# Quarter additions on GpSimd between gathers, and a slot's work in two steps, in a two-layer graph network kernel

## The chip, the cores and the metric

The kernel runs on one core of a Trainium2 chip. Time is the device time of one launch in microseconds (us), the median of several runs: 2489.55 us before the change, over 11 runs from 2482.47 to 2493.50. Engines are named as in the profile: PE is the matrix engine (PEld its weight loads), DVE the vector engine, ACT the scalar engine, POOL is GpSimd, SP the engine that only issues DMAs.

## The reference

6250 nodes with 512 features, 100000 edges sorted by destination, eight heads of 64 features. Two layers, each added to its input:

```python
h = jnp.maximum(_layernorm(x, axis=-1), 0.0)
# edge layer 0: attention
h = leaky_relu(h @ W.T + b, 0.2).reshape(N, 8, 64)
e = leaky_relu(e_src[src] + e_dst[dst], 0.2)      # e_* : sums of h times a weight, per head
ex = jnp.exp(e - segment_max(e, dst)[dst])
a = ex / segment_sum(ex, dst)[dst] * dist
x = x + segment_sum(h[src] * a[:, :, None], dst)
h = jnp.maximum(_layernorm(x, axis=-1), 0.0)
# edge layer 1: mean of neighbours
neigh = segment_sum(h[src], dst) / deg
y = h @ W_self.T + neigh @ W_neigh.T + bias
x = x + _layernorm(y) * gamma + beta
```

## The kernel before

A prologue computes `h` and the two logit terms for 49 tiles of 128 nodes and stores rows of 520 numbers in DRAM. Then come the two edge layers, the bulk of the time.

**Edges.** The edge list is cut into four streams (q = 0 to 3), and each stream into 66 windows of three tiles (j = 0 to 2) of 128 edges. In each window twelve tiles are gathered: an indirect DMA on GpSimd's queue fetches, for 128 edges, the rows of their sources. GpSimd runs its instructions in the order in which they are written; a gather is an instruction on it like an addition. In the first layer (`gather`, L744) the rows land in `gbuf`, a ring of four windows: the gather for window k+4 overwrites the buffer of window k, tile by tile, once PE has used that tile. In the second (`gather1`, L1296) the tiles of half a window land in a ring of five.

**Products.** PE turns gathered rows into sums per destination with one-hot matrices (`add_up`, L1010; `add_up1`, L1325), adds what is carried from the window before (`finish`), and ACT copies the result out (`evac`), from where SP stores it.

**Messages (first layer).** Before PE uses a tile, its rows are multiplied in place by the attention weights: by DVE two streams at a time for the tiles j = 0 and 1 (`message`, L967), for the third tile in part by DVE (`message_part`, L974) and in groups of four heads by ACT (`message_act`, L986, four 128x64 activations a group). The upper four heads of streams 1 and 3 in that tile are left to GpSimd (`message_pool`, L998, steps `K0` and `K1`, one 128x256 multiplication each), except in the last two full windows.

**Order.** All engines' instructions are written out by hand: for each window k the list `ORDER` is gone through, and each name calls a function for window k plus an offset (`STEPS`). GpSimd's part of a window is K0, six gathers of window k+4 (`GA`), K1, the other six (`GB`). The tiles follow in the order `TILES` (stream, tile): 10 01 00 30 11 20 02 22 12 21 31 32.

**Slots.** 128 finished rows are a slot. Slots follow some windows (six windows of every seven, from window 9 on; 49 of them, of which the last belongs with six further ones to a late group that is handled at the end of a layer). In the first layer `slot_load` fetches the sums (`sa`) and the input (`sx`) of the slot of window k-2; `slot_run`, for the slot of window k-3, goes on by one step at each `S` of the order: divides by the softmax sums (DVE, L1088), adds `sx` and `sa` (DVE, 128x512, L1090), takes statistics (L1101), scales and stores the normalised rows. In the second layer `slot1_run` does the two dense products and the closing normalisation; its last lines add `beta` to `sx` (L1475), multiply by `gamma` (L1477) and add (L1478), on DVE but for the last two slots before the late ones.

**Buffers.** `sa0` has two buffers in the first layer, `sx` three; the penalties that separate destinations in the softmax (`penb`) four, loaded by `load_edges` four windows ahead.

Of the kernel before, what the change touches and what calls it, by code (L numbers as in the profile page):

```python
# [1 line left out]

# [17 lines left out]
NQ = 4  # L20
# [24 lines left out]
def gnn_kernel(ctx, tc, x, srcp, dstp, attrp, wt0, b0, wsrc, wdst, wts, wtn, bias1, gamma1, beta1, out):  # L45
# [673 lines left out]
    gp = lay0.enter_context(tc.tile_pool(name="gp", bufs=1))  # L719
    penb = [gp.tile([NQ * H, T * 128 + 1], FT, name=f"penb{i}") for i in range(4)]  # L720
    gbuf = gp.tile([128, NB, NQ, T, RW], FT, name="gbuf")
# [13 lines left out]

    def gather(k, part=None):
        GT[k] = g_ = gbuf[:, k % NB]
        tiles = [(q, j) for q, j in TILES if j < njof(k)]
        if k >= NW - 3:
            tiles.sort(key=lambda t: t[1])  # L740
        n = len(tiles) // 2
        for q, j in tiles if part is None else (tiles[:n], tiles[n:])[part]:
            c = k * T + j
            G.indirect_dma_start(out=g_[:, q, j, :], out_offset=None, in_=h0_d,  # L744
                                 in_offset=bass.IndirectOffsetOnAxis(ap=idx[:, q, c:c + 1], axis=0))

    def attr_turn(k, h):
# [24 lines left out]
    def load_edges(k):  # L772
        n = njof(k) * 128
        for p in (1, 0):
            if p == 0 and k % GRP[1]:
                continue
            eb = ed_tile(k, p)
            for q2 in range(2):
                S.dma_start(eb[64 * q2:64 * q2 + 64, (2 * p + q2) * H:(2 * p + q2 + 1) * H], ed_d[ds(base(k, 2 * p + q2), M), :])
        PEN[k] = pn = penb[k % 4]  # L780
        S.dma_start(pn[:, 0:n + 1], pen_d[:, k * T * 128:k * T * 128 + n + 1])
# [211 lines left out]

    def message_pool(k, p):

        if njof(k) == T and not (p and k in IDLE):
            x3 = GT[k][:, 2 * p + 1, T - 1, D // 2:D].rearrange("p (h d) -> p h d", d=D // H)
            G.tensor_tensor(out=x3, in0=x3, in1=A2[k][:, T - 1, 2 * p + 1, H // 2:H].unsqueeze(2).to_broadcast([128, H // 2, D // H]),  # L998
                            op=OP.mult)

    def add_up(k, p, j):
# [70 lines left out]
    def slot_load(s, r=None):  # L1072
        if r is None:
            r = load(tab[0:1, s:s + 1], NP - 128)
        sa = lp.tile([128, AW], FT, name="sa0")
        S.dma_start(sa, acc0_d[ds(r, 128), :])
        sx = lp.tile([128, D], FT, name="sx", bufs=3) if s + 1 != LATE[0] else keep[:, LATES]
        S.dma_start(sx, x[ds(r, 128), :])
        SA[s] = (r, sa, sx)
# [12 lines left out]

    def slot_run(s, engs=(V, V)):
        r, sa, sx = SA.pop(s)
        V.tensor_scalar(slc[:, s, 0:H + 1], sa[:, D:AW], 1.0, None, op0=OP.max)
        yield
        V.reciprocal(slc[:, s, 0:H + 1], slc[:, s, 0:H + 1])
        yield
        yield from residual(s, sa, sx, engs)
        s6 = lp.tile([128, 6], FT, name="s6_0")  # L1100
        V.bn_stats(s6, sx)  # L1101
        yield
        mv = lp.tile([128, 2], FT, name="mv_0")
        V.bn_aggr(mv, s6)
        yield
        y = yield from rstd_of(lp, mv[:, 1:2], 1, "s0", slc[:, s, 9:10])
        V.scalar_tensor_tensor(slc[:, s, 10:11], mv[:, 0:1], -1.0, y, op0=OP.mult, op1=OP.mult)
        yield
        A.activation(sx, sx, AF.Relu, scale=y, bias=slc[:, s, 10:11])
        if s + 1 == LATE[0]:  # L1110
            DONE.append((r, sx))
        else:
            S.dma_start(h1_d[ds(r, 128), :], sx)
# [38 lines left out]

    def ahead(k, part):
        if k >= NB - 1:
            gather(k, part)


# [10 lines left out]
        A10=(0, add_up, 1, 0), A11=(0, add_up, 1, 1), A12=(0, add_up, 1, 2), C0=(0, finish, 0), C1=(0, finish, 1),  # L1168
        EV0=(0, evac0), EV1=(-1, evac1), OH=(4, onehot), CS=(0, later(carry_sel)),
        GA=(NB, ahead, 0), GB=(NB, ahead, 1), K0=(0, message_pool, 0), K1=(0, message_pool, 1))  # L1170
    STEPS.update({f"H{p}{i}": (0, message_act, p, i) for p in range(2) for i in range(4) if p or i})
    ORDER = """
    K0 H01 D0b S D0a D1a TE ECb H11 NX S SCR S FT1 A00 D0c FL EV1 SV S H12 RESC A01 AT0 H02 OH TM A10 GA K1 S CM FDf
    A02 FX S RS S LM RH AT0c CS SSb C0 SUB PF L FT1c S EZ EXP D1b SCF S A11 H10 AT1 ECa AT1c FT0 S AA F9a S A12 F9b S
    EV0 FD SSa C1 FT0c S GB
    """.split()
# [8 lines left out]
    for k in range(-4, NW + 1):  # L1185
        sl_ = slot_run(slot(k - 3)) if slot(k - 3) is not None and slot(k - 3) not in LATE else none()
        c, kk = divmod(k, CH)
        when(k + 4, load_edges)
        if slot(k - 2) is not None and slot(k - 2) not in LATE:
            slot_load(slot(k - 2))  # L1190
        if kk == CH - 6 and 0 <= k and (c + 1) * CH < NW:
            attr_load(c + 1)
        for name in ORDER:
            if name[0:2] == "AT":
                (attr_copy if name[3:] else attr_turn)(k, 4 * int(name[2]))
            elif name == "S":
                step(sl_)
            elif name == "L":
                step(last)
            else:  # L1200
                d, f, *a = STEPS[name]
                when(k + d, f, *a)
        if NW - 6 < k <= NW - 2:
            for i in range(2 * (k - NW + 5), min(2 * (k - NW + 6), LATES)):
                late_x(i)
        last = sl_


    late_sa = gbuf[:, (NW - 4) % NB].rearrange("p q j r -> p (q j r)")[:, 0:LATES * AW].rearrange("p (i c) -> p i c", c=AW)
    for i, s_ in enumerate(LATE):  # L1210
        S.dma_start(late_sa[:, i], acc0_d[ds(ROW[s_], 128), :])
    run(last)
    for r, hs in DONE:
# [77 lines left out]
    def gather1(k, p):  # L1291
        GT[k, p] = g_ = ring[:, (2 * k + p) % 5]
        for j in range(njof(k)):
            for q2 in (1, 0):
                c = k * T + j
                G.indirect_dma_start(out=g_[:, q2, j, :], out_offset=None, in_=h1_d[0:NT * 128, :],  # L1296
                                     in_offset=bass.IndirectOffsetOnAxis(ap=idx[:, 2 * p + q2, c:c + 1], axis=0))

    lay1 = ExitStack()
# [133 lines left out]
    def slot1_mean(s):  # L1433
        sa = SA[s][3]
        if s not in OWN:
            A.activation(sa, sa, AF.Copy, scale=slc[:, s, 8:9])

    def slot1_run(s):
        r, hs, sx, sa = SA.pop(s)
# [34 lines left out]
        eng = G if LATE[0] - 2 <= s < LATE[0] else V  # L1474
        eng.tensor_tensor(out=sx, in0=sx, in1=gb[:, 1], op=OP.add)  # L1475
        yield
# [93 lines left out]
    STEPS1.update({f"A{p}{j}": (0, add_up1, p, j) for p in range(2) for j in range(T)})  # L1570
    SLOTS1 = dict(MEAN=(-2, slot1_mean), SUMS=(-1, slot1_sums))
    ORDER1 = """
    en en la MEAN A00 A01 A02 la A10 CS0 C0 EV1 OH en PUT en PRE G1 sl la SEL en en SUMS CS1 sl A11 A12 EV0 G0 C1 sl
    """.split()

    last, ends = none(), none()
    for k in range(-1, NW - 1):
# [5 lines left out]
        for name in ORDER1:  # L1583
# [14 lines left out]
            elif k >= 0 or name[0] != "G":  # L1598
                d, f, *a = STEPS1[name]
                when(k + d, f, *a)  # L1600
        if 12 <= k < 12 + NLATE:
            late_beta(k - 12)
# [192 lines left out]
```

## Time and profile before

| | |
|---|---|
| median of 11 runs | 2489.55 us |
| profiled execution, own time | 2492.52 us |
| its span, first to last instruction | 2490.7 us |
| granted clock of PE, mean | 0.923 |
| first layer, first gather's start to last gather's end | 225.8 to 1327.7 us |
| second layer, the same | 1406.5 to 2425.6 us |

The profile is of one execution. A group's row has the line, the engine, the operation, its output and inputs with shapes, the count, the busy time and the mean of one, and the idle time of that engine just before, with what ended it ("issue" is idle time in which the engine waited for nothing that the profile shows). The timeline has one row for each instruction or run of like ones.

### The profile page before, as it was taken

To read this page: it belongs to the slowest core of one execution; us is meant where nothing else is said; L and a number is where in the kernel's file an instruction comes from. 1 tells how busy PE (TensorE), PEld (TensorE's weight loads), DVE (VectorE), ACT (ScalarE), POOL (GpSimd) and SP (SyncE) were. 2 spreads that over 40 slices of the span, in tenths; PEclk is the share of its full clock that TensorE was granted. 3 is DMA by queue.
4 is the path that set the end of the run, shared out by engine and by line. 5 is a ranking of instruction groups with operands and counts; after the bars stand their busy time and mean duration, and the time that the engine had idled before them with its cause. 6 is when DMAs were issued, how large, how long until landed. Compare 5 with 4: busy or idle time off the path is not lost.

```text
span 2490.7 us, 32878 instructions
## 1 busy us (share of the span) xinstructions
PE 2068.6 (83%) x8780; PEld 1017.9 (41%) x8780; DVE 1539.4 (62%) x3120; ACT 984.9 (40%) x2957; POOL 1813.9 (73%) x1803
## 2 busy tenths in 40 slices
PE   7985799888888888898889277898888879888885
PEld 5774244333333333343334033344444434444344
DVE  7877566676867776867778422365545545555545
ACT  6862344555545555545554311222222222222212
POOL 5665777777777777777774477777777777777773
PEclk9997799999999999999999599899989999999898
DMA  6735777788888888888886688888888888888882
GB/s 208 226 92 158 211 220 213 233 271 242 260 257 262 255 261 258 256 257 250 258 254 189 212 250 256 269 284 281 282 276 288 284 276 285 281 284 277 289 272 85
DMA packets 264702, 611.54 MB, mean 246 GB/s; under 512 B 63604, under 2 KB 74372, under 8 KB 264510
## 3 DMA queue, kind: packets, MB, share of 16 engines
q0 software_dynamic: 125440, 414.35, 55.8%
q1 hardware_dynamic: 138494, 193.97, 23.6%
q8 instruction: 72, 1.18, 0.2%
q14 instruction: 120, 0.98, 0.1%
q10 hardware_dynamic: 576, 1.05, 0.1%
HBM read 511.44 MB, written 97.76 MB: 245 GB/s over the span
## 4 chain that ended last, share of the span: by engine, by line
PE 32%; DMA 22%; POOL 21%; issue 13%; DVE 8%; ACT 3%; SPq 1%; POOLq 0%; ACTq 0%; DVEq 0%
DMA g<-h_d,idx 15%; POOL gbuf L744 11%; POOL g L1296 8%; PE ps_w L1010 7%; PE ps_w L1325 4%; DMA gbuf<-h_d,idx 4%; PE ps_z L818 3%; PE ps_f L592 3%; PE ps_s L1325 2%; PE ps_b L592 2%; PE ps_w L592 2%; POOL gbuf L998 1%; PE ps_w L1027 1%; PE ps_z L827 1%; PE ps_f L1018 1%
## 5 line engine op out<-in xcount | busy, mean ns | idle before, releaser
L744 POOL DMA_INDIRECT gbuf<-h_d,idx x784 | 781.4, 997 | 249.1 <-issue 154.3
L1296 POOL DMA_INDIRECT g<-h_d,idx x784 | 780.5, 996 | 243.3 <-issue 182.5
L1010 PE MATMUL ps_w<-gbuf,oh 128*64 128x512 f32 x1568 | 491.6, 630 | 126.4 <-POOL gbuf L998 105.0
L986 ACT ACTIVATE gbuf<-gbuf,aa 128x64 f32<-128x64 f32 x1276 | 329.6, 334 | 1.6
L1325 PE MATMUL ps_s<-g,oh 128*64 128x512 f32 x784 | 213.2, 659 | 123.0 <-DMA g<-h_d,idx 75.3
L967 DVE TENSOR_TENSOR gbuf<-gbuf,ps_c 128x1024 f32<-128x1024 f32 x260 | 308.4, 1215 | 0.3 <-issue 0.3
L1325 PE MATMUL ps_w<-g,oh 128*64 128x512 f32 x784 | 219.0, 650 | 78.0 <-DMA g<-h_d,idx 77.3
L1010 PEld LDWEIGHTS ps_w<-gbuf,oh 128*64 128x64 f32 x1568 | 97.4, 137 | 249.6 <-POOL gbuf L998 179.2
L854 DVE TENSOR_TENSOR_SCAN nx<-penb,ms,ps_z 32x256 f32<-32x256 f32 x66 | 48.2, 730 | 208.2 <-PE ps_z L827 199.2
L1423 ACT ACTIVATE hs<-sx,slc 128x512 f32<-128x512 f32 x45 | 36.6, 814 | 352.8 <-PE ps_t L1406 212.7
L628 POOL TENSOR_TENSOR pr<-hr,watt 128x1024 f32<-128x1024 f32 x47 | 113.2, 2411 | 77.6 <-DVE hr L625 71.1
L1038 ACT ACTIVATE ws<-ps_w 128x512 f32<-128x512 f32 x103 | 60.6, 588 | 272.3 <-PE ps_w L1027 270.1
L1325 PEld LDWEIGHTS ps_s<-g,oh 128*64 128x64 f32 x784 | 47.9, 143 | 245.2 <-DMA g<-h_d,idx 135.1
L1412 DVE TENSOR_TENSOR lo<-ps_t,hi 128x512 fp32r<-128x512 f32 x55 | 38.0, 690 | 158.0 <-ACT hi L1411 157.5
L787 DVE TENSOR_TENSOR oh<-ps_c,dsr 128x768 f32<-128x768 f32 x130 | 123.0, 947 | 0.1
L818 PE MATMUL ps_z<-oht,edb 128*32 128x384 f32 (+1 forms) x264 | 121.6, 593 | 1.1 <-DVE mf L847 1.1
L1325 PEld LDWEIGHTS ps_w<-g,oh 128*64 128x64 f32 x784 | 43.0, 140 | 182.6 <-DMA g<-h_d,idx 127.4
L1027 PE MATMUL ps_w<-ws,cs 128*128 128x512 f32 x170 | 97.3, 654 | 0.0
L998 POOL TENSOR_TENSOR gbuf<-gbuf,aa 128x256 f32<-128x256 f32 x128 | 82.2, 643 | 19.3 <-DVE slc L198 17.2
L1345 ACT ACTIVATE ws<-ps_w 128x512 f32<-128x512 f32 x66 | 39.2, 594 | 137.6 <-PE ps_w L1333 122.2
L806 PE MATMUL ps_t<-ident,oh 128*128 128x128 f32 x392 | 73.9, 298 | 14.2 <-DVE oh L787 12.3
L810 ACT ACTIVATE oht<-ps_t 128x384 f32<-128x384 f32 x132 | 63.1, 478 | 53.4 <-PE ps_t L806 53.3
(398 smaller groups left out, 3947.2 us busy)
## 6 DMA issues: line engine op xcount, KB each, us to landing
sx<-x SPq DMA_DIRECT2D x95, 256.0 KB
acc_d<-ws SPq DMA_DIRECT2D x182, 130.2 KB
acc_d<-ws SPq DMA_DIRECT2D x182, 128.0 KB
h_d<-hr SPq DMA_DIRECT2D x49, 260.0 KB
gbuf<-h_d,idx POOLq DMA_INDIRECT x784
g<-h_d,idx POOLq DMA_INDIRECT x784
sa<-acc_d SPq DMA_DIRECT2D x48, 260.5 KB
s<-acc_d SPq DMA_DIRECT2D x48, 256.0 KB
```

What stands on the lines that cost most here:

```text
L592: P.matmul(pt, a_[:, k], w_[:, k], start=not last[0], stop=stop and k == 3 and w_ is whi_ and a_ is lo)
L628: G.tensor_tensor(out=pr, in0=hr[:, None, 0:D].to_broadcast([128, 2, D]), in1=watt, op=OP.mult)
L744: G.indirect_dma_start(out=g_[:, q, j, :], out_offset=None, in_=h0_d, in_offset=bass.IndirectOffsetOnAxis(ap=idx[:, q, c:c + 1], axis=0))
L787: V.tensor_tensor(out=oh.rearrange("p a j b n -> p (a j b) n"), in0=c_iota[:, None, :].to_broadcast([128, 4 * T, M]), in1=dsr[:, k].rearra ...
L818: P.matmul(z[0:NQ * H, 0:n], ed_tile(k, p), oht[:, p, 0:n], start=(p == 0), stop=False, skip_group_check=True)
L967: eng.tensor_tensor(out=x4, in0=x4, in1=(AA if eng is V else A2)[k][:, i, q].unsqueeze(3).to_broadcast([128, 2, H, D // H]), op=OP.mult)
L986: A.activation(x_, x_, AF.Copy, scale=A2[k][:, T - 1, 2 * p + q2, h:h + 1])
L998: G.tensor_tensor(out=x3, in0=x3, in1=A2[k][:, T - 1, 2 * p + 1, H // 2:H].unsqueeze(2).to_broadcast([128, H // 2, D // H]), op=OP.mult)
L1010: P.matmul(w[r, :], oh[:, p, j, q2], g_[:, 2 * p + q2, j, 0:D], start=(j == 0 and not goes_on(k, p)), stop=False, skip_group_check=True)
L1027: P.matmul(w, CS[k][:, p], c[:, p, 0:D], start=False, stop=True, skip_group_check=True)
L1296: G.indirect_dma_start(out=g_[:, q2, j, :], out_offset=None, in_=h1_d[0:NT * 128, :], in_offset=bass.IndirectOffsetOnAxis(ap=idx[:, 2 * p ...
L1325: P.matmul(BK[p][64 * q2:64 * q2 + 64, :], OHs[k][:, p, j, q2], GT[k, p][:, q2, j, :], start=(j == 0 and not goes_on(k, p, 1)), stop=False ...
```

## The change

GpSimd's multiplications K0 and K1 go; ACT gets the two groups of heads back (`H03`, `H13`). The gathers of a window are issued in one go after the order's list, and after each third gather GpSimd takes one piece from a list `PAUSE`, if there is one: a quarter (128x128) of an addition in place. In the first layer the quarters are those of `sx + sa`, which leave DVE; the slot's work is split in two: `slot_run` (for window k-3) ends where it has put the four quarters on the list, and `slot_end` (for window k-4, so one window later) takes statistics and stores. At the steps `S` of a window `slot_end` of the older slot comes first (its statistics at the first `S`, right after `D0b`), then `slot_run` of the younger one (its division at the eleventh `S`, after `AA`; at the third where no older slot is open). `sa0` gets a third buffer, and `penb` gives one up and is loaded a window later. In the second layer the quarters are those of `sx + beta` (step `BETA`, which leaves DVE), taken after the third and the sixth gather of each half window. What is left on the list when the gathers end is done at once.

```diff
+    PAUSE = []
+    def pause():
+        if PAUSE:
+            x_, y, c = PAUSE.pop(0)
+            G.tensor_tensor(out=x_[:, c], in0=x_[:, c], in1=y[:, c], op=OP.add)
+    def quarters(x_, y):
+        PAUSE.extend((x_, y, slice(c, c + D // 4)) for c in range(0, D, D // 4))
-    def gather(k, part=None):
+    def gather(k):
...
-        n = len(tiles) // 2
-        for q, j in tiles if part is None else (tiles[:n], tiles[n:])[part]:
+        for i, (q, j) in enumerate(tiles):
             c = k * T + j
             G.indirect_dma_start(...)
+            if i % 3 == 2:
+                pause()
...
-        PEN[k] = pn = penb[k % 4]
+    def load_pens(k):
+        n = njof(k) * 128
+        PEN[k] = pn = penb[k % 3]
         S.dma_start(pn[:, 0:n + 1], pen_d[:, k * T * 128:k * T * 128 + n + 1])
...
-    def message_pool(k, p):
...
-        sa = lp.tile([128, AW], FT, name="sa0")
+        sa = lp.tile([128, AW], FT, name="sa0", bufs=3)
...
-        yield from residual(s, sa, sx, engs)
+        sa3 = sa[:, 0:D].rearrange("p (h d) -> p h d", h=H)
+        V.tensor_copy(c_rec[:, 0:H], slc[:, s, 0:H])
+        V.tensor_tensor(out=sa3, in0=sa3, in1=c_rec[:, 0:H].unsqueeze(2).to_broadcast([128, H, D // H]), op=OP.mult)
+        quarters(sx, sa)
+        SA[s] = (r, sx)
+    def slot_end(s):
+        r, sx = SA.pop(s)
         s6 = lp.tile([128, 6], FT, name="s6_0")
         V.bn_stats(s6, sx)
...
     ORDER = """
-    K0 H01 D0b S D0a D1a TE ECb H11 NX S SCR S FT1 A00 D0c FL EV1 SV S H12 RESC A01 AT0 H02 OH TM A10 GA K1 S CM FDf
-    A02 FX S RS S LM RH AT0c CS SSb C0 SUB PF L FT1c S EZ EXP D1b SCF S A11 H10 AT1 ECa AT1c FT0 S AA F9a S A12 F9b S
-    EV0 FD SSa C1 FT0c S GB
+    H13 H01 D0b S D0a D1a TE ECb H11 NX S SCR S FT1 A00 D0c FL EV1 SV S H12 RESC A01 AT0 H03 H02 OH TM A10 S CM FDf A02
+    FX S RS S LM RH AT0c CS SSb C0 SUB PF L FT1c S EZ EXP D1b SCF S A11 H10 AT1 ECa AT1c FT0 S AA F9a S A12 F9b S EV0
+    FD SSa C1 FT0c S
...
-        sl_ = slot_run(slot(k - 3)) if slot(k - 3) is not None and slot(k - 3) not in LATE else none()
+        early_, sl_ = (f(slot(w)) if slot(w) is not None and slot(w) not in LATE else none()
+                       for w, f in ((k - 3, slot_run), (k - 4, slot_end)))
+        sl_ = chain(sl_, early_)
...
         when(k + 4, load_edges)
+        when(k + 3, load_pens)
...
-        last = sl_
+        run(sl_)
+        if k >= -1:
+            when(k + NB, gather)
+        if k + NB >= NW - 1:
+            while PAUSE:
+                pause()
...
     def gather1(k, p):
...
+                if (j, q2) in ((1, 1), (2, 0)):
+                    pause()
...
+    def slot1_beta(s):
+        BETA.add(s)
+        quarters(SA[s][2], gb[:, 1])
...
-        eng.tensor_tensor(out=sx, in0=sx, in1=gb[:, 1], op=OP.add)
+        if s not in BETA:
+            eng.tensor_tensor(out=sx, in0=sx, in1=gb[:, 1], op=OP.add)
...
-    en en la MEAN A00 A01 A02 la A10 CS0 C0 EV1 OH en PUT en PRE G1 sl la SEL en en SUMS CS1 sl A11 A12 EV0 G0 C1 sl
+    en en la MEAN A00 A01 A02 la A10 CS0 C0 EV1 OH en PUT en PRE BETA G1 sl la SEL en en SUMS CS1 sl A11 A12 EV0 G0 C1 sl
```

## The prediction

> **What bounds the kernel now.** I read the page's busy rows and groups first, then busy time by stretch, then GpSimd's timeline, its groups by form, and last DVE's timeline beside GpSimd's.
>
> The page, one row per engine, and three groups (line, engine, operation, count | busy us, mean ns | idle before, releasers):
>
> ```profile
> PE 2068.6 (83%) x8780; PEld 1017.9 (41%) x8780; DVE 1539.4 (62%) x3120; ACT 984.9 (40%) x2957; POOL 1813.9 (73%) x1803
> L744 POOL DMA_INDIRECT gbuf<-h_d,idx x784 | 781.4, 997 | 249.1 <-issue 154.3
> L1296 POOL DMA_INDIRECT g<-h_d,idx x784 | 780.5, 996 | 243.3 <-issue 182.5
> L998 POOL TENSOR_TENSOR gbuf<-gbuf,aa 128x256 f32<-128x256 f32 x128 | 82.2, 643 | 19.3 <-DVE slc L198 17.2
> ```
>
> The shares name PE, but the two gather groups with the idle time before them hold 2054 us of GpSimd. By stretch (gathers of the first edge layer, then of the second):
>
> ```profile
> core 0: us, PE busy (x) PEld busy (x) DVE busy (x) ACT busy (x) POOL busy (x), PEclk, DMA share, GB/s
> 225.80:1327.70 1101.90, 947.54 (x4164) 408.50 (x4164) 779.41 (x1529) 555.66 (x2059) 861.17 (x908) 0.94 0.84 247
> 1406.50:2425.60 1019.10, 852.64 (x3425) 414.96 (x3425) 491.43 (x1043) 232.00 (x441) 780.54 (x784) 0.93 0.87 278
> ```
>
> GpSimd's timeline in the first layer (start us, us, what, idle before):
>
> ```profile
> 1006.50 0.94 POOL L744 DMA_INDIRECT gbuf<-h_d,idx  x1 [0.30 <-issue]
> 1007.46 0.63 POOL L998 TENSOR_TENSOR gbuf<-gbuf,aa 128x256 f32<-128x256 f32 x1
> 1008.25 0.99 POOL L744 DMA_INDIRECT gbuf<-h_d,idx  x1 [0.16 <-issue]
> 1009.54 0.95 POOL L744 DMA_INDIRECT gbuf<-h_d,idx  x1 [0.30 <-PE ps_w L1010]
> ```
>
> Each gather is followed by 0.30 us of idle time, whatever the bracket names: a beat of 0.946+0.304 = 1.25 us. In the second layer 783 of 784 idle times are this one; 741.7 (784x0.946), 238 (783x0.304) and 38.9 of stretched gathers are its 1019 us. The first layer's 1101.9 is 741.7+238, 34.4 stretched, 75.5 for 124 messages (below) and 13 of waiting for PE. **Both layers run at GpSimd's beat.** From every twelfth gather, a window of the first layer takes 16.95 us (mean of the last 49).
>
> **The price of a piece.** From 1006.50 to 1008.25 is 1.75 us instead of 1.25: the message's 0.625 (median), 0.017 ahead of it, an idle time of 0.159 for 0.304, and a next gather of 0.989 for 0.946. So d us cost d-0.085: 0.54; the mean over the 124 that stand between gathers is 0.61, as some meet a busy DVE. A 128x128 sum of two full tensors is in no row. The nearest:
>
> ```profile
> L1475 POOL TENSOR_TENSOR sx<-sx,gb 128x512 f32<-128x512 f32 x2 | 2.6, 1282 | 0.0
> L382 POOL TENSOR_TENSOR dsr<-dstt,bbs 128x195 f32<-128x195 f32 x4 | 2.2, 543 | 0.0
> L384 POOL TENSOR_TENSOR dsr<-dstt,bbs 128x1 f32<-128x1 f32 x4 | 0.8, 195 | 0.0
> ```
>
> A straight line from 1 to 512 elements gives 0.195+127x0.0021 = 0.46; I take d = 0.45, as the 195 row lies a little under the line. Below: the 195 row in proportion, 0.36. Above: 0.195+128x1.282/512 = 0.52. So 0.365, and 0.05 for a busy DVE: **0.415 us**, bounds 0.27 and 0.50.
>
> The Trainium skill (GPSIMD Engine Reference, 3.1 and 4.1) speaks against the change: it calls this engine the wrong one for ordinary sums. It gives 4497 ns for 2048 elements; in plain proportion that is an estimate of 0.28 for 128, so 0.20 a piece, and the sum below would fall by some 38 us in the second layer.
>
> **Second layer.** In: 44 slots have their quarters among the gathers, and two more pieces: 178x0.415 = +74. Out: DVE's 46 additions of 0.686 us. DVE is busy half the time there, but it holds gathers up:
>
> ```profile
> 1976.63 1.04 POOL L1296 DMA_INDIRECT g<-h_d,idx  x1 [0.30 <-issue]
> ```
>
> ```profile
> 1976.16 0.68 DVE L1475 TENSOR_TENSOR sx<-sx,gb 128x512 f32<-128x512 f32 x1
> ```
>
> A gather that starts while DVE adds two tensors from SBUF ends 0.82 us after the sum (1976.84 to 1977.67). Put to DVE's lines in this way, 7.0 of the 38.9 us belong to L1475: -7. The Trainium skill (SBUF — State Buffer, "Who interferes with whom") infers that `tensor_tensor` does not hold up descriptor generation; by that the 7 would be no gain, and the rows decide. DVE's closing addition waits for the last quarter, a window and a half after the list is filled; behind it wait the next slot's residual and the split of the carry, and for that PE's closing product. GpSimd reuses a buffer only five half windows later: nothing. **Sum +67.**
>
> **First layer, without its waits.** Out: 124x0.61 = 75.5. In: 169 quarters among the gathers, 70.1. Waiting for PE -9 of 13, DVE's addition stretched eight gathers, -1.5. ACT's eight activations more (0.333 each, 2.7 us a window) find an engine busy 8 to 10 of 17 us. SP's later loads and stores are covered by a window each. This alone would be -16, and -4 at the end, as PE would follow closer.
>
> **The new waits.** The statistics of a slot stand on DVE at the first step of window k+1, right behind `D0b`; they need all four quarters, the last behind the twelfth gather of window k+4. The quarters need the division, DVE's eleventh step in window k. GpSimd's first and last gather of window 47 (k = 43), then DVE in window 44:
>
> ```profile
> 1016.93 0.99 POOL L744 DMA_INDIRECT gbuf<-h_d,idx  x1 [0.16 <-DVE s_v L185]
> ...
> 1031.96 0.95 POOL L744 DMA_INDIRECT gbuf<-h_d,idx  x1 [0.30 <-issue]
> ```
>
> ```profile
> 1021.57 1.22 DVE L967 TENSOR_TENSOR gbuf<-gbuf,ps_c 128x1024 f32<-128x1024 f32 x1
> 1022.70 0.17 DVE L1095 TENSOR_SCALAR slc<-sa 128x9 f32<-128x9 f32 x1
> 1027.87 0.73 DVE L854 TENSOR_TENSOR_SCAN nx<-penb,ms,ps_z 32x256 f32<-32x256 f32 x1 [2.74 <-PE ps_z L827]
> 1037.46 0.34 DVE L903 TENSOR_TENSOR ps_c<-ex,at 128x96 f32<-128x96 f32 x1
> ```
>
> DVE is at that first step at 1022.7, and the last gather of 47 ends at 1032.9: ten us of wait. The eleventh step follows L903, near 1038, just when window 48's third gather ends (1033.7 and three beats): once DVE is ten us later, GpSimd waits there in turn. That does not settle by a shift, it is **a ring**: division (k), four quarters with nine gathers between, statistics (k+1), most of DVE's window, division (k+1).
>
> GpSimd's half: four pieces of 0.45, nine gathers (three times 0.989+0.946+0.946), gaps (three times 0.159+0.304+0.304+0.017): 12.8.
> DVE's half, from the last quarter: statistics 0.71, messages `D0a` and `D1a` 2.35, scan 0.73, aggregate 0.18, scan 1.0, variance 0.16: 5.2 with handing over. Now ACT, in its order: logarithm and exponential 0.45, then three groups of heads (twelve in 2.95; they stand behind these two): 8.7, copy 0.33 (L878): 9.05. DVE again: leaky, carry selector, subtraction, scale 1.0, message `D1b` 1.2, scan 0.95: 12.2 (PE's product, logit sum and ACT's copy are done at 10.6). Maximum, reciprocal, weights, division 0.35+0.5+0.83: 13.85.
> Ring: 13.85+12.8+0.15 = **26.8 us** for a window. Bounds: 24.6 if ACT's three groups come ahead of the exponential (DVE's work alone then sets 11.5), 28.2 if PE, idle half the time, runs at a lower clock (0.55 to 0.79 granted in the first windows, where it is idle too) and its 1.4 us of products come on the path.
>
> Five of seven windows are linked like this. The other two (no older slot, or no younger) go by the beat and by the release of buffers: 5.5 until `A01` has freed the second tile, 14.4 for the rest, 16.7 for the next twelve with four quarters: 37. Seven windows take 5x26.8+37 = 171 instead of 118.7. From window 13 to 62: six such groups and a seventh in which few gathers are left (134+28): 1188. Before, products of 13 start at 506.0 and of 62 at 1330.8: 825. **+363.** The twelve windows without slots ahead gain 13, but the first wait takes 8 back: -5. Four windows at the end, where quarters follow one another without gathers: +6. The last slot's statistics lie in DVE's idle 9.35 us ahead of the late rows. Sum +364; the -16 is in the beat used here.
>
> **Total:** 364+67 = +431. The profiled execution took 2492.5 (span 2490.7), so 2923.5; it is 3 us over the median of 2489.55, so **2920 us**.
>
> **The rivals.**
> *A. The ring does not close*: statistics wait for less than I read. Then the beat sets all: +67-20, 2537. For it: PE has 9 to 16 us between the landing of rows and their first use. Against: that slack moves a wait, it does not open a ring.
> *B. No ring, and small pieces are cheap*, which ends on the other side. Saved are 75.5+9+1.5+4+7 = 97, so 347 pieces break even at 0.28 each; at 0.15, 2445. For it: 195 elements took only 0.54. Against: the one-element row, and the 0.16 us behind each message.
> *C. The second layer closes up too*: PE, fully busy in several windows there, waits for the carry behind DVE's closing addition; at 2 us in 44 windows, 3010.
> *That it doesn't do what it says*: additions could pile up past the gathers; but four enter and four places exist in each window with a slot.
>
> **How the numbers follow.** Forecast 0.74; its own range 2815 to 2985 (ring 24.6 to 28.2 in 35 windows, -77 to +49; pieces, -26 to +15). A 0.09, B 0.05, C 0.12. About 0.2% (5 us) is what a measurement of this kernel tells from no change. Faster 0.04, same 0.01 (both B), slower 0.95. The range leaves out A and B: 2800 to 3010.
>
> **What would show it.** In the first layer, windows with gathers in the pattern of three, a pause of some 6 us, then three times a piece and three gathers; that pause put to DVE's division, and DVE's largest wait at the statistics (L1101) for GpSimd; PE's clock lower; windows before the first slot near 15.5 us. In the second, gaps of 0.16 behind pieces of 0.45 and a stretch of some 1086 us. Wrong if the first layer's windows stay under 18 us, or if GpSimd's idle time does not name DVE.

## The result, and the profile after

The changed kernel takes 3000.85 us (median of 8 runs, 2993.73 to 3005.11), the kernel before 2488.44 us (31 runs, 2479.93 to 2493.50) on the same chip: a ratio of 1.2058, 95% interval 1.2045 to 1.2072. The forecast was 2920 us in a range of 2800 to 3010, of which its own terms gave 2815 to 2985. The profiled execution has a span of 2997.5 us and a mean granted clock of 0.814 (2490.7 and 0.923 before).

| us of the span | before | after | difference | forecast |
|---|---|---|---|---|
| first layer, first gather's start to last one's end | 1101.9 | 1535.7 | +433.8 | +364 |
| from there to the second layer's first gather | 78.8 | 82.7 | +3.9 | 0 |
| second layer | 1019.1 | 1086.2 | +67.1 | +67 |
| behind it | 65.1 | 67.3 | +2.2 | 0 |

Lines of `kernel.py` have moved: the gathers are now L755 and L1317, GpSimd's quarters L743, the statistics L1118, the division L1110, PE's first-layer products L1019. The page after, busy row and groups:

```profile
PE 2174.8 (73%) x8780; PEld 1103.3 (37%) x8780; DVE 1473.2 (49%) x3026; ACT 1101.9 (37%) x3469; POOL 1901.6 (63%) x2054
L755 POOL DMA_INDIRECT gbuf<-h_d,idx x784 | 770.5, 983 | 529.9 <-PE ps_w L1019 316.9
L1317 POOL DMA_INDIRECT g<-h_d,idx x784 | 782.6, 998 | 218.0 <-issue 169.6
L1118 DVE BATCH_NORM_STATS2 s<-sx 128x6 f32<-128x512 f32 x47 | 32.6, 694 | 505.8 <-POOL sx L743 505.8
L743 POOL TENSOR_TENSOR sx<-sx,sa 128x128 f32<-128x128 f32 x188 | 86.0, 460 | 202.2 <-issue 177.1
```

No engine is nearly full any more. The statistics are 47 instructions of 0.7 us, and DVE stood idle for 505.8 us ahead of them, all of it put to GpSimd's quarters; GpSimd stood idle for 202.2 us ahead of quarters and, in the first layer, 529.9 ahead of gathers (249.1 before). Busy time by stretch, first layer and second:

```profile
core 0: us, PE busy (x) PEld busy (x) DVE busy (x) ACT busy (x) POOL busy (x), PEclk, DMA share, GB/s
225.70:1761.40 1535.70, 1037.75 (x4166) 465.11 (x4166) 734.17 (x1479) 671.41 (x2559) 848.44 (x953) 0.75 0.60 177
1844.10:2930.30 1086.20, 867.64 (x3421) 443.72 (x3423) 473.49 (x996) 230.03 (x441) 870.37 (x965) 0.89 0.83 260
```

GpSimd's own work in the first layer went down (861.17 to 848.44 us), DVE's too (779.41 to 734.17), and the layer takes 434 us more: it is waiting, not work. PE does the same products, for 1037.75 us instead of 947.54, at a clock of 0.75 instead of 0.94.

One turn of the ring. GpSimd (start us, us, what, idle before), from one slot's first quarter to the next one's:

```profile
1212.00 0.47 POOL L743 TENSOR_TENSOR sx<-sx,sa 128x128 f32<-128x128 f32 x1
1212.63 1.07 POOL L755 DMA_INDIRECT gbuf<-h_d,idx  x1 [0.16 <-issue]
1214.00 0.95 POOL L755 DMA_INDIRECT gbuf<-h_d,idx  x1 [0.31 <-issue]
...
1224.44 0.47 POOL L743 TENSOR_TENSOR sx<-sx,sa 128x128 f32<-128x128 f32 x1
1229.09 1.26 POOL L755 DMA_INDIRECT gbuf<-h_d,idx  x1 [4.18 <-PE ps_w L1019]
1233.63 0.94 POOL L755 DMA_INDIRECT gbuf<-h_d,idx  x1 [3.28 <-PE ps_w L1019]
1234.88 1.02 POOL L755 DMA_INDIRECT gbuf<-h_d,idx  x1 [0.30 <-issue]
1241.19 0.45 POOL L743 TENSOR_TENSOR sx<-sx,sa 128x128 f32<-128x128 f32 x1 [5.30 <-issue]
```

The same turn on DVE:

```profile
1224.93 0.69 DVE L1118 BATCH_NORM_STATS2 s<-sx 128x6 f32<-128x512 f32 x1 [10.73 <-POOL sx L743]
...
1234.22 0.36 DVE L901 SCALAR_TENSOR_TENSOR et<-ps_b,et 128x192 f32<-128x192 f32 x1 [2.95 <-ACT et L894]
...
1238.40 1.00 DVE L863 TENSOR_TENSOR_SCAN mf<-penb,mf,ps_z 32x384 f32<-32x384 f32 x1 [2.13 <-ACT e L857]
...
1240.37 0.69 DVE L1110 TENSOR_TENSOR sa<-sa,ps_c 128x512 f32<-128x512 f32 x1
```

PE:

```profile
1226.80 1.97 PE L1019 MATMUL ps_w<-gbuf,oh 128*64 128x512 f32 x4 [8.25 <-DVE gbuf L983]
1228.71 2.75 PE L1027 MATMUL ps_f<-ex,oh 128*128 128x18 f32 x12
1231.38 1.98 PE L1019 MATMUL ps_w<-gbuf,oh 128*64 128x512 f32 x4
...
1238.11 1.08 PE L1019 MATMUL ps_w<-gbuf,oh 128*64 128x512 f32 x4
```

Read them in order of time. GpSimd's four quarters with nine gathers between last from 1212.00 to 1224.91; 0.02 us later DVE takes the statistics; the division ends at 1241.06 and the next first quarter starts at 1241.19. GpSimd's half of the ring is 12.9 us, DVE's 16.3. PE's rows show what is in the second half and was not in the forecast: after 8.25 us of idle time four products take 1.97 us, at 1238 again 1.08. The clock record says the same, half speed from 1220.5 to 1237.6. DVE's two waits, 2.95 for ACT's copy of the logits and 2.13 for the copy behind PE's logit sum, lie behind these slow products.

### The profile page after: what moved, and what is told of

It is laid out like the page before. It is cut to its first block, busy times and chain, and to the rows that moved or that the text cites. A ratio compares the mean times of both kernels' runs of the same rounds, so it can differ in the third digit from the quotient of the medians.

```text
span 2997.5 us, 33617 instructions
## 1 busy us (share of the span) xinstructions
PE 2174.8 (73%) x8780; PEld 1103.3 (37%) x8780; DVE 1473.2 (49%) x3026; ACT 1101.9 (37%) x3469; POOL 1901.6 (63%) x2054
## 5 line engine op out<-in xcount | busy, mean ns | idle before, releaser
L755 POOL DMA_INDIRECT gbuf<-h_d,idx x784 | 770.5, 983 | 529.9 <-PE ps_w L1019 316.9
L1317 POOL DMA_INDIRECT g<-h_d,idx x784 | 782.6, 998 | 218.0 <-issue 169.6
L1019 PE MATMUL ps_w<-gbuf,oh 128*64 128x512 f32 x1568 | 543.6, 791 | 457.2 <-DVE gbuf L983 442.1
L1002 ACT ACTIVATE gbuf<-gbuf,aa 128x64 f32<-128x64 f32 x1788 | 451.0, 333 | 0.5
L1019 PEld LDWEIGHTS ps_w<-gbuf,oh 128*64 128x64 f32 x1568 | 105.3, 167 | 558.8 <-DVE gbuf L983 452.6
L1118 DVE BATCH_NORM_STATS2 s<-sx 128x6 f32<-128x512 f32 x47 | 32.6, 694 | 505.8 <-POOL sx L743 505.8
L743 POOL TENSOR_TENSOR sx<-sx,sa 128x128 f32<-128x128 f32 x188 | 86.0, 460 | 202.2 <-issue 177.1
L1509 DVE TENSOR_TENSOR o<-o,sx 128x512 f32<-128x512 f32 x46 | 31.9, 693 | 258.1 <-POOL sx L743 258.0
L1356 PE MATMUL ps_w<-chi,cs 128*128 128x512 f32 x65 | 39.5, 608 | 154.2 <-DVE chi L1379 154.2
L901 DVE SCALAR_TENSOR_TENSOR et<-ps_b,et 128x192 f32<-128x192 f32 x66 | 23.5, 356 | 181.4 <-ACT et L894 181.3
L834 PE MATMUL ps_z<-oht,edb 128*32 128x384 f32 (+1 forms) x264 | 99.3, 500 | 1.1 <-DVE mf L863 1.1
L863 DVE TENSOR_TENSOR_SCAN mf<-penb,mf,ps_z 32x384 f32<-32x384 f32 (+1 forms) x65 | 64.4, 991 | 68.5 <-ACT e L857 68.0
L743 POOL TENSOR_TENSOR sx<-sx,gb 128x128 f32<-128x128 f32 x188 | 92.3, 492 | 3.4
```

The costliest lines, as they stand in the source:

```text
L743: G.tensor_tensor(out=x_[:, c], in0=x_[:, c], in1=y[:, c], op=OP.add)
L834: P.matmul(z[0:NQ * H, 0:n], ed_tile(k, p), oht[:, p, 0:n], start=(p == 0), stop=False, skip_group_check=True)
L1002: A.activation(x_, x_, AF.Copy, scale=A2[k][:, T - 1, 2 * p + q2, h:h + 1])
L1019: P.matmul(w[r, :], oh[:, p, j, q2], g_[:, 2 * p + q2, j, 0:D], start=(j == 0 and not goes_on(k, p)), stop=False, skip_group_check=True)
```

## The experiments

They ran on two chips on which the kernel before itself takes 2722 to 2746 us instead of 2488 (the chip of the result is called the first chip here); what the traces show of that stands at the end. So each is set against before, and against the changed kernel, on such a chip. "DVE half" is from the start of a slot's statistics to the start of the next slot's first quarter, "GpSimd half" from a first quarter's start to its fourth's end, "turn" the time between first quarters; means of the 35 linked turns (five windows in each of seven groups). "Half clock" is the time for which PE's clock was at half speed in a linked window (mean).

| kernel | DVE half | GpSimd half | turn | half clock | first layer | second layer | ratio to before |
|---|---|---|---|---|---|---|---|
| changed, first chip | 15.74 | 12.98 | 28.75 | 17.7 | 1535.7 | 1086.2 | 1.2058 |
| changed | 15.65 | 13.18 | 28.86 | 17.4 | 1603.3 | 1147.8 | 1.1524 |
| quarters every second gather | 15.36 | 9.24 | 24.64 | 12.7 | 1419.3 | 1144.3 | 1.0838 |
| quarters together | 20.40 | 1.70 | 22.71 | 7.5 | 1354.6 | 1152.7 | 1.0553 |
| 16 idle products | 14.60 | 13.10 | 27.73 | 6.9 | 1564.4 | 1157.1 | 1.1377 |
| 22 idle products | 14.00 | 13.08 | 27.12 | 3.3 | 1532.1 | 1141.6 | 1.1293 |
| order of slots swapped | no ring | 14.02 | 18.39 | 4.9 | 1254.0 | 1156.2 | 1.0176 |
| before | | | | 3.3 | 1191.3 | 1150.1 | 1 |

The two halves and the handing over between them (0.03 us; 0.61 on average with the quarters together) follow one another by definition, so their sum proves nothing. That the ring is closed is seen at its two joints: in the first six kernels the statistics start 0.03 us behind the fourth quarter (with the quarters together in 28 of the 35 turns), and in all 35 turns the next first quarter starts 0.08 to 0.14 us behind the end of the division. In the swapped order it starts 6.9 us behind it on average, and never less than 1.4.

### The changed kernel and the kernel before again

> The changed kernel itself, unaltered, beside the same runs of before as the other kernels of this call, so that these can be set against it. Theory (the ring of DVE's and GpSimd's halves sets the first layer on any chip): linked windows of 28 to 29.5 us as in the first profile; the second layer's gathers stretch is bounded by something other than GpSimd's beat where before takes about 2745 us, near 1157 us with or without the pieces: 3170 us (3130 to 3210), ratio 1.14 to 1.17 there; 3000 us and 1.206 where before takes 2488. Rival (the first layer too is bounded by late handovers there, and the ring is hidden behind them): the ratio is under 1.10 there.

> The kernel before itself, for its trace on the chip of this call. If before takes about 2745 us there: the gathers themselves last 0.95 us as in the first profile, the second layer's stretch is 1145 to 1160 us instead of 1019, the first layer's near 1200 instead of 1102, and the difference is idle time of GpSimd ahead of single gathers, about one of 2 to 4 us every 18 us in the second layer. Rival: each gather or each gap is longer by a constant.

The changed kernel took 3136.44 us (4 runs; before 2721.92, 7 runs): 1.1524, interval 1.1495 to 1.1553, inside the expected 1.14 to 1.17. Linked windows are 27.8 to 30.9 us, on the first chip 27.8 to 31.8. The kernel before took 2730.67 us; its first layer 1191.3 us and its second 1150.1. Its gathers last no longer than on the first chip (0.98 us on average); what has grown is the idle time ahead of them, as its page shows:

```profile
L1296 POOL DMA_INDIRECT g<-h_d,idx x784 | 769.5, 981 | 385.4 <-issue 201.0
L744 POOL DMA_INDIRECT gbuf<-h_d,idx x784 | 770.8, 983 | 332.9 <-issue 176.8
```

Together 718 us instead of 492: 226 of the 238 us by which its span is longer. Against it, the change costs 412 us in the first layer and nothing in the second. So the first layer's loss is much the same on either chip (412 and 434 us), and the second's is not.

### Swapping the slots' order: the ring opened

```diff
-        sl_ = chain(sl_, early_)
+        sl_ = chain(early_, sl_)
```

Now `slot_run` of the younger slot goes first in a window and `slot_end` of the older one behind it; the division no longer stands behind the older slot's statistics. Every instruction is still there.

> Ring theory: the changed kernel's first layer is set by the ring division (window k, DVE's eleventh step) - four quarters with nine gathers between - statistics (window k+1, first step). With the younger slot's steps first, the division is DVE's third step and the statistics come behind it at the same step, so a division no longer waits for the quarters of the window before; what is left spans two windows (12.9 us of pieces and gathers and about a window of DVE, under 30 us for two) and is shorter than two beats of GpSimd (2 x 16.6). The first layer's gathers then take some 1085 us as the beat without waits gives, not 1536, and the whole 2540 us (2515 to 2575). Rival (work, not order: the quarters' cost, the port shared with DVE, ACT's eight activations more): the work is the same, so the time stays near 3000 us.

> The changed kernel with the slot's early half (its statistics and what follows) ahead of the late half in the same step, so that a slot's division no longer stands behind the next slot's statistics. Theory (the ring): the ring is open, each slot has a window more, and both layers go at GpSimd's beat: second layer still +67 us (178 pieces), first layer about -16 to -4 against before: 2540 us (2515 to 2575) on a chip where before takes 2488, ratio 1.02. On a chip where before takes about 2746 because gathers wait elsewhere: ratio 1.01 to 1.025. Rival (the pieces and their stretched gathers themselves cost the time, or DVE is the bound): near 3000, ratio 1.20.

2792.47 us (before 2745.81): 1.0176, interval 1.0143 to 1.0208; the second time 2790.26: 1.0162, 1.0133 to 1.0190. Both lie in the 1.01 to 1.025 that the second expectation gives for such a chip. (It has the two parts' names turned round: the edit puts the younger slot's division ahead of the older slot's statistics.) DVE's idle time ahead of the statistics is 158.8 us on its page (493.9 in the changed kernel on that chip):

```profile
L1118 DVE BATCH_NORM_STATS2 s<-sx 128x6 f32<-128x512 f32 x47 | 32.6, 693 | 158.8 <-issue 131.8
```

The first layer takes 1254.0 us instead of 1603.3. So 349 of its 412 us go with the order in which DVE is given the two parts of a slot's work, and the rival, that pieces and stretched gathers cost the time, falls: they are all still in. What is left over before, 63 us, is not the -16 to -4 of the forecast's "without its waits"; the windows at the ends of a group of slots are the long ones (20 to 23 us). Whether that is the quarters or these chips was not separated.

### Fewer gathers between the quarters

```diff
-            if i % 3 == 2:
+            if i % 2 == 1 and i < 8:
```

> The changed kernel with a slot's quarters behind the 2nd, 4th, 6th and 8th gather of the window instead of the 3rd, 6th, 9th and 12th: the same pieces, six gathers between first and last instead of nine. Theory (the ring): GpSimd's half shrinks by three gathers with their gaps, 3 x 1.25 = 3.75 us, so linked windows fall from 28.7 to 25 (24.4 to 25.6) and 35 of them take 131 us less than the changed kernel on the same chip (105 to 150), a ratio to before lower by 0.04 to 0.055. Rival (the time is in the pieces, in stretched gathers or in DVE's own work, of which nothing changes): within 20 us of the changed kernel.

2951.07 us: 1.0838, interval 1.0810 to 1.0865. GpSimd's half fell by 3.9 us and DVE's stayed within 0.3; windows, first gather to first gather, fell from 28.7 to 24.5, as forecast. In all it is 185 us less than the changed kernel, more than the 105 to 150 expected: the linked windows give 35 x 4.2 = 147, and the two windows at a group's ends lost some 5 us together in each of seven groups, which the expectation had left out.

```diff
-            if i % 3 == 2:
-                pause()
+            if i == 2:
+                for _ in range(4):
+                    pause()
```

> The changed kernel with the four quarters of the first layer one behind another after the third gather (same additions, same count, same order of a slot's steps). Ring theory: GpSimd's half of the ring shrinks from 12.9 to about 2 us, DVE's half stays (14 to 16.3), so a linked window takes 16.5 to 18.5 instead of 28.7, the first layer's gathers some 1150 us instead of 1536, and the whole 2615 us (2560 to 2680). Rival (work, not order): same pieces, same time as the changed kernel, near 3000 us.

2898.18 us (before 2745.81): 1.0553, interval 1.0530 to 1.0576. GpSimd's half is 1.70 us, but the turn is 22.7, not the beat's 17: DVE's half has grown to 20.4. The waits of ACT (line waited for: us in total, times, longest) say where:

```profile
ACT et L895 <- remote: 223.6, 35, 9.5
```

"Remote" means that the profile finds nobody who ended the wait. These are 35 waits of 6.4 us on average ahead of the copy of the logits, in 27 of the 35 linked turns: 5.1 us a turn. In the turn that ends at 1214.3, PE's transposes that the copy waits for end at 1200.9, and the copy starts at 1209.2; no count of PE's is recorded between 1204.62 and 1209.06, and then six within 0.24 us (PE's counts that land late, last section). The size of the turn was missed, 22.7 us for 16.5 to 18.5: without these waits DVE's half would be some 15.3 us, inside the 14 to 16.3 that were expected. What delays the counts was not forecast and stays open.

### Keeping PE's clock up

In 43 windows, the linked ones among them, PE gets products of 128x256 that nobody reads, into a free part of a PSUM bank (PE's output memory), while it would wait for the slot's statistics:

```diff
         src = (E_, MR)[i][k]
+        if i == 0 and slot(k - 5) is not None and slot(k - 5) not in LATE and k < NW - 2:
+            for _ in range(16):
+                P.matmul(PB[k][:, 256:512], ident, iota, start=True, stop=True, skip_group_check=True)
```

> The changed kernel with 16 further products of 128x256 on PE, into a part of PSUM that nothing reads, given out at the first step of each linked window, while PE waits for the slot's statistics; it computes the same. Theory (the half of the ring on DVE is 2.4 us longer than forecast because PE, idle for eight to nine us, runs its first products at half speed): PE stays at full speed, A-products near 1.08 us for four of them instead of 1.97, the ring falls from 28.7 to 26.5 to 27.2 us, 35 linked windows less 1.5 to 2.2 us each: 2920 to 2950 us where before takes 2488, ratio 1.175 to 1.186. Rival (the 2.4 us are ACT's or DVE's own, or the slow products lie beside them): 2990 to 3010, ratio 1.20 to 1.21. Second rival: the throttle takes the clock back for the added products: above 3010.

> As the version with 16 idle products in each linked window, with 22, so that PE is idle for under 1.5 us ahead of its first products instead of 3.8 us. Theory (PE's half clock after idle time is what made DVE's half 16.3 us instead of 13.85): with 16 the linked window was 27.25 us and the clock at half speed for 6.8 us of it; with 22 it does not fall, and linked windows are 26.2 to 26.9 us, 35 windows x 0.35 to 1.0 = 12 to 35 us less than with 16 products: 3085 to 3110 where that one took 3121, ratio 1.125 to 1.133. Against the changed kernel on the same chip 65 to 90 us less. Rival (what is left over 26.8 is ACT's or DVE's own): 27.25 again, 3115 to 3130. Second rival (the added products come in the way of the slot's own): longer.

With 16 it takes 3121.31 us (before 2744.19): 1.1377, interval 1.1333 to 1.1421; with 22, 3073.95 us (before 2721.92): 1.1293, 1.1258 to 1.1329. Against the changed kernel's 1.1524 that is 40 and 63 us less, though PE is given more to do (2531.2 us busy with 22, 2208.7 in the changed kernel). PE's timeline with 22, in a window in which it stayed at full clock (its first-layer products are L1022 here; the added ones are the last row, in which each stands as two records, some of them missing):

```profile
892.79 1.08 PE L1022 MATMUL ps_w<-gbuf,oh 128*64 128x512 f32 x4 [0.82 <-DVE gbuf L986]
893.80 1.51 PE L1030 MATMUL ps_f<-ex,oh 128*128 128x18 f32 x12
895.25 1.08 PE L1022 MATMUL ps_w<-gbuf,oh 128*64 128x512 f32 x4
...
906.88 8.45 PE L890 MATMUL ps_b<-iota,ident 128*128 128x256 f32 x38
```

The first two rows took 1.97 and 2.75 us in the changed kernel. Windows like this one take 26.05 to 26.11 us (13 of 35), DVE's half 13.2. In the same execution the 15 linked windows with over 6 us at half clock take 27.2 to 28.3 us. So the time goes with the clock, from kernel to kernel and from window to window, and that the clock lengthens DVE's half is shown. The gains fell a little short of the expected 50 to 81 us with 16 and 65 to 90 with 22: the mean window is 27.5 and 26.5, and some starts of groups got longer.

### The second layer's quarters alone, and the messages alone

First, before with the second layer's part of the change alone (`pause`, `quarters` and `slot1_beta` as in the diff above):

```diff
+                if (j, q2) in ((1, 1), (2, 0)):
+                    pause()
...
-        eng.tensor_tensor(out=sx, in0=sx, in1=gb[:, 1], op=OP.add)
+        if s not in BETA:
+            eng.tensor_tensor(out=sx, in0=sx, in1=gb[:, 1], op=OP.add)
```

Second, before with the first layer's messages moved and nothing else:

```diff
-    K0 H01 D0b S D0a D1a TE ECb H11 NX S SCR S FT1 A00 D0c FL EV1 SV S H12 RESC A01 AT0 H02 OH TM A10 GA K1 S CM FDf
+    H13 H01 D0b S D0a D1a TE ECb H11 NX S SCR S FT1 A00 D0c FL EV1 SV S H12 RESC A01 AT0 H03 H02 OH TM A10 GA S CM FDf
```

> The kernel before with the second layer's part of the change alone (beta added in quarters among the gathers). Price of a piece 0.38 us less what DVE's additions had stretched: second layer's gathers 1086 instead of 1019 us, the whole 2556 us (2545 to 2570), first layer unchanged. Rival (part of the second layer's loss comes from the first layer's change, through later stores or a shifted phase): under half of the 67 us, below 2525.

> The kernel before with the second layer's quarters alone (first layer untouched). Theory (178 pieces at 0.415 us, less 7 us of gathers that DVE's sum no longer stretches): +67 us, 2556 (2545 to 2570) where before takes 2488, ratio 1.027, the second layer's gathers stretch 1086 instead of 1019. Rival (the pieces are hidden in the gap behind a gather): under 2525, ratio under 1.015. On a chip where before takes about 2746 and GpSimd waits some 2.5 us about every 18 us in the second layer: ratio 1.000 to 1.005, as the pieces lie in those waits.

> The kernel before with one part of the change alone: GpSimd's two multiplications of a window go to ACT, no quarters, slots as before, gathers where they were. Ring theory: nothing of this part is in the ring, so it only takes 124 x 0.61 us and some of the waiting for PE out of GpSimd's beat: a window of the first layer 15.4 to 15.6 us instead of 16.95, the whole 2400 us (2385 to 2430). Rival (ACT's load is part of the loss): copies that PE waits for come late behind ACT's new groups, no gain or a loss, 2480 to 2560 us.

> The kernel before with the messages of the first layer on ScalarE alone (no quarters in either layer, order of slots unchanged). Theory (GpSimd's beat is the limit of both layers): 124 messages at 0.61 us and 9 us of waits go, 8 more activations on ACT in each window find it half idle: 2400 (2385 to 2430) where before takes 2488, ratio 0.965; windows of the first layer near 15.5 instead of 16.95. Rival (ACT, or PE behind it, becomes the bound of the first layer): 2480 to 2560, ratio 0.997 to 1.03. On a chip where before takes about 2746: ratio 0.997 to 1.003.

Quarters alone: 2747.18 and 2742.94 us, 1.0003 (0.9992 to 1.0014) and 1.0002 (0.9984 to 1.0020). Messages alone: 2750.46 and 2749.72 us, 1.0004 (0.9986 to 1.0022) and 1.0019 (1.0003 to 1.0036). The first expectation of each is of a chip on which GpSimd's beat is the bound; here it isn't. The second ones, with a figure for these chips, hold. In the second layer GpSimd's waits beyond its ordinary gap number 77 in before, 142 us in all; with 93 us of quarters between the gathers they are 58, 82 us: most of the pieces lie in time that was lost anyway. The layer is 9 us longer than in the trace of before, but so is the first layer (10 us), which was not changed, and the whole kernel is not slower. Likewise the messages that leave GpSimd leave more idle time behind. So neither the +67 us nor the gain of a lighter GpSimd could be tried where the beat holds; the first rests on the trace of the changed kernel alone, the second stays open. No kernel tried is faster than before.

## Why the prediction was nearly right

The measured 3000.85 us lie in the stated range, but above the 2985 to which the ring's and the pieces' bounds reached. The range went to 3010 for rival C, which did not happen; so that the time lies inside is in part luck, while the mechanism is the one forecast.

**The ring.** Right: where it closes, which instruction waits (L1118, 505.8 us), that five windows of seven are linked, that PE's clock falls (0.75 in the first layer, 0.94 before), that windows without slots come to 15.5 (mean of the first sixteen 15.52). The swapped order shows that it is the ring and not the work.

**The ring's size.** 26.8 us forecast, 28.75 measured. GpSimd's half was 12.8 and is 12.98; the handing over 0.15 and is 0.03; DVE's half was 13.85 and is 15.74. The mis-sized term is PE's lower clock. The prediction named it, priced it at 1.4 us as an upper bound and left it out of the value. It is not only 1.4 us of products that come on the path: DVE waits for ACT, ACT for transposes (L889), and the transposes stand behind four large products, twelve small ones and four large ones again, all at half speed. From the first of these to the third group's end it took 6.6 us in the turn shown, and 3.5 at full clock in the window with 22 idle products. At full clock the turn is 26.1, which is 2.65 us under the changed kernel's, and DVE's half 13.2, somewhat under the 13.85 that was added up from rows. So the bound of 28.2 was too low, and the sum without the clock 0.7 too high. (The 26.1 is from another chip; the changed kernel's turn is 28.86 there.)

**The first layer's sum.** +433.8 for +364. Of the 70 us too few, 35 x (28.75 - 26.8) = 68 are the ring; the other two windows of a group took 39.3 instead of 37, 14 in six groups. Against that, the sixteen windows ahead of the first slot's wait gained 17 instead of 13, that wait cost 3.5 instead of 8 (the 17th window took 20.4, before 16.9), and some 4 us are left over at the layer's end, not traced. The 6 us between and behind the layers were put at nothing.

**The second layer.** 1086.2 us as forecast, by two errors that cancel, which is luck. The quarters took 87.8 us (180 pieces, 0.488 on average, 0.46 undisturbed, forecast 0.45) and the gaps shrank by 22.8: 65 instead of 74. But the 7 us of stretched gathers did not come back: the stretching is 40.9 us, before 38.9. One piece and the gathers behind it, from GpSimd's timeline after:

```profile
2500.21 0.46 POOL L743 TENSOR_TENSOR sx<-sx,gb 128x128 f32<-128x128 f32 x1
2500.82 0.97 POOL L1317 DMA_INDIRECT g<-h_d,idx  x1 [0.16 <-issue]
2502.10 0.95 POOL L1317 DMA_INDIRECT g<-h_d,idx  x1 [0.30 <-issue]
```

Each such gather is itself 0.02 longer, 179 times. The rest is kept up by the change itself. DVE's closing addition (L1509, before L1478) now waits for the slot's last quarter, starts 0.03 us behind it, and so always meets the next gather; DVE's row and the two of GpSimd:

```profile
2508.92 0.69 DVE L1509 TENSOR_TENSOR o<-o,sx 128x512 f32<-128x512 f32 x1 [7.32 <-POOL sx L743]
```

```profile
2508.42 0.46 POOL L743 TENSOR_TENSOR sx<-sx,gb 128x128 f32<-128x128 f32 x1
2509.04 1.40 POOL L1317 DMA_INDIRECT g<-h_d,idx  x1 [0.16 <-issue]
```

The gather takes 1.40 to 1.41 us instead of 0.95, in all 45 slots. Put to DVE's lines as the prediction did, the closing addition stretches gathers by 20.7 us after 13.6 before: that is the 7 us. It waits long itself (258.0 us ahead of L1509), but GpSimd waits for nothing behind it, as the prediction said.

**The rivals.** A (no ring) is out by 505.8 us; B by the piece's 0.46 us. C, that the second layer closes up: PE does wait long for the carry, on the page after

```profile
L1356 PE MATMUL ps_w<-chi,cs 128*128 128x512 f32 x65 | 39.5, 608 | 154.2 <-DVE chi L1379 154.2
```

but no idle time of GpSimd between two of the second layer's gathers or pieces is above 0.35 us, so it cost nothing.

**A sign that was put wrongly.** "Wrong if GpSimd's idle time does not name DVE": it names PE (316.9 us ahead of gathers) and "issue" (177.1 ahead of quarters), and DVE's division for 9.4 of the 202.2 us. The pause that was expected as one of 6 us, at the quarter, is three: 4.18 and 3.28 us for buffers that PE frees late, then 5.30. The name in the bracket is that of the last event near the end of the wait; the end of L1110, 0.13 us ahead of the quarter, shows who released it.

## What to carry to other kernels

A list of instructions written out by hand makes an order on each engine. Before work is handed from one engine to another and back, draw the circle: if the piece that comes back stands on the first engine ahead of what the next round needs, one round's time is the sum of both halves, however idle the engines are. Swapping two steps opened it here and took 349 us away. And price the halves with PE at half clock, if the circle makes it idle: here 2.65 us of each 28.75.

## What the runs showed of the hardware

**PE's clock after idle time.** In the changed kernel's first layer, after idle times of 7.5 to 13.1 us, the half clock set in 1.3 to 4.7 us after PE's last product, and full clock returned 7.9 to 11.2 us after PE had started again (42 times); in before, after idle times of 2.4 to 3.3 us, 2.9 to 5.9 us after. It is not the length of the idle time that makes the return late: in the changed kernel's second layer, after idle times of 5.2 to 9.8 us, full clock returned 3.1 to 6.5 us after the start (15 times). By the records PE is busy without a pause in these 8 to 11 us too; what differs is its products (in the first layer, as in PE's rows above, weights of 64 columns and products of 18 columns; in the second, behind the 9.8 us, products of 128x512 with weights of 128 columns). Which of it counts was not tried. The Trainium skill (TensorE: Matmul & The Clock Gate, Part 1) gives at least one window of some 3.4 us for either way. For the way up the second layer's records come near it, and the first layer's are two to three times as long. For the way down 34 of the 42 half clocks set in less than 3.4 us after PE's last product, so the window before them was not idle throughout.

**Counts of PE that land late.** In the trace of before on a chip of the experiments GpSimd stops ahead of 77 gathers of the second layer, for 2.1 us on average; its timeline there:

```profile
2306.77 0.95 POOL L1296 DMA_INDIRECT g<-h_d,idx  x1 [0.30 <-issue]
2308.03 1.42 POOL L1296 DMA_INDIRECT g<-h_d,idx  x1 [0.30 <-issue]
2311.72 0.95 POOL L1296 DMA_INDIRECT g<-h_d,idx  x1 [2.27 <-remote]
2312.97 0.95 POOL L1296 DMA_INDIRECT g<-h_d,idx  x1 [0.30 <-issue]
```

Engines tell each other what is done by counts (semaphores), and the trace records when a count lands. On the first chip nine in ten of PE's counts land within some 0.05 us of a product's end. Here none lands from 2306.30 to 2311.37, and then seven within 0.26 us; the gather follows 0.09 us later. Four or more counts within 0.25 us after a silence of over 1.5 us occur 92 times in before there (median silence 5.1 us), never in either trace of the first chip. Such silences stand ahead of 22 of ACT's 34 long waits with the quarters together, too. That they make up the 238 us by which before is longer there was not added up: 40 of the 92 lie in the second layer, which has the 77 stops. These traces also lack a part of the count records (1975 of PE's instead of 2419), so a silence alone could be missing records, and the profile can say "remote"; the gather that follows a burst at once speaks for counts that land late. What holds them up, and why on these chips, stays open.
